# A two-layer kernel: second batch's norm statistics, normalised tiles, gating and last layer's weights put in other slots of the row loop

## The chip, the cores and the metric

One core of a Trainium2 chip runs the whole kernel in one launch. A core has a matrix engine (PE, with weight loads shown as PEld), a vector engine (DVE), an activation engine (ACT), a general engine (POOL) and a queue engine that issues transfers (SP). The metric is the device time in microseconds, and the figure for a kernel is the median of several runs.

## The reference, cut to what matters

The input x has 2 batches of 1024 rows of 512 numbers. There are two layers, and each layer adds an attention part and a second part, both computed from the same normalised input:

```python
x = L0_attn_x
xn = _layernorm(x)
x = x + L0_attn(xn) + L0_ffn(xn)      # one head of 128; streams mixed by a 4x4 Sinkhorn matrix per row
xn = _layernorm(x)
x = x + L1_attn(xn) + L1_ffn(xn)      # 32 heads in 8 groups, causal; gated experts of rank 16
```

In `L0_ffn` each row's 512 numbers are 4 streams of 128. A matrix `H_res` per row (50 rounds of row and column normalisation of 16 logits) mixes the streams, and a small branch is added. `L1_attn` projects to 32 query heads and, over a latent of 4 x 128 columns, to 8 key and value heads; scores are masked causally. `L1_ffn` is a gate and a product:

```python
h = relu(layernorm(xf @ gw1.T + gb1) * ln_gamma + ln_beta)
gates = h @ gw2.T + gb2
top_v, top_i = top_k(gates, 2);  top_g = softmax(top_v)
counts = onehot(top_i).sum(0);   allowed = counts <= capacity     # over both batches
w = onehot * top_g * allowed
out = xf @ weight.T + lora_B(lora_A(xf) * w) / 16
```

The counts run over all 2048 rows, so that no routing weight is known before both batches have been gated.

## The kernel before, in words

All matrix products are made of 16-bit halves: a float32 operand is split into a high and a low part, and `mm3` (line 88) sums three products, high by high, high by low, low by high. A split of activations is a high part on ACT and a low part on DVE (`evac`, lines 104 and 105); a split of weights is three POOL instructions (`split_pool`, lines 94 to 96: a scaling, a high part, a low part).

A tile is 128 rows of x; a batch has 8. `acc[b, t]` holds the running sum of tile t of batch b. Layer 0 of both batches comes first (`front0`, `attn0_rows`, `branch0`, `attn0_out`), with the mixing of the first batch's streams and its second norm. Then comes `layer1_attn`, which is most of the time.

`layer1_attn` runs over 16 groups g (8 of the first batch, then 8 of the second) and 32 row steps s in each. A row step takes 32 query rows of 4 heads against the keys so far (`row_step`): score matmuls on PE (tile `s`, 32 to 1024 columns), a row minimum on DVE (lines 283 and 287, into `P`), the exponential on ACT (line 291), a reciprocal (302), the high part on ACT (308) and the low part on DVE (314), both into `Phl`, and a transpose by DMA on SP (line 320, `PT<-Phl`). Rows lag: `row_step` finishes the row before the one whose scores it starts. `last_low` names the newest low part. In the first 8 rows of a group four rows share a `P` and a `Phl` buffer, in the next 8 rows two do, later each has its own; POOL sets the unused columns of `Phl` to zero (line 319).

All else is put between row steps. `at(g, s, f)` and `put(h, s, f)` name the slot after which a piece is written down; `put` counts from `8 * h`, so slot 200 is group 6, row 8. Group work has fixed slots: keys and values, query projections (`xT` by `wq`, evacuated at lines 104 and 105), the products with the transposed rows (`av`, line 345), and the output projection (`wo_block`), whose result is added to `acc` at line 737 on DVE, which frees its `pp` buffer; there are three of those (`BP`). The slots of what is not group work are in the constants at the top: `SK0, SKN` the second batch's Sinkhorn steps, `MX0, MXN` its mixing, `LN1` its second norm, `G0` and `G1` the gating of the first and second batch with `GL` slots between a tile and its gating matmul, `WT` the routing weights, `LX` the tiles of the second batch's `xT`, `LA` its latents, `FW` the last layer's weights, `FF` its first blocks. All of these lie in groups 0 to 7.

The order within each engine's queue is then set by the scheduler of the language, from what is written in the slots and from dependencies; it may put an instruction earlier or later than its slot. Two helpers bind it: `tc.issue_after`, and `behind(i, j, wait)`, which puts i behind j, with `wait` through a semaphore even across engines. POOL's weight splits (`parts_of`, `ffn_split`) and the adds of the mixing (line 634) wait in this way for the newest low part.

What the change touches:

- `mix0_units(1, t, ...)`: loads x again, scales it on POOL (617), and for each of 4 streams makes four ACT copies scaled by `Hm` (633) and one POOL add into `acc` (634).
- `layernorm_tiles`: `bn_stats` and an aggregation per tile (219, 220), then a square root by logarithm and exponential with corrections (`rsqrt`), and the scales `rs` (223, 224), for all 8 tiles in slot `LN1`.
- `normed_T`: scales a tile (`pool` chooses DVE 237, POOL 235 or ACT 233), its high part on ACT (238), its low part on POOL (240) or DVE, and a DMA transpose on SP (242). `tile_of` does this for the second batch's gating, scaling on POOL into `f2k` with high and low parts in `xr` (4 buffers) and the result in a `wo` buffer; the transposed tiles are dropped after gating, because `xT` (one buffer) still holds the first batch. `xT_tile` does it again when `xT` is free.
- `gating_h`: 12 matmuls of 32 columns (`gw`) and one DVE instruction (864) per tile; `gating`: DVE work for all 8 tiles in ten steps (lines 868 to 913).
- `weights_of`: sums the counts of both batches with a matmul (919) and makes the routing weights on DVE (921 to 929). `ffn_block`: one tile of the last product.
- `lat_w`, `ffn_fetch`, `ffn_split`: loads on POOL's queue and splits of the latent and last layer's weights.

## Time and profile before

| what | us |
|---|---|
| median of 3 runs (lowest to highest) | 1857.18 (1856.16 to 1858.09) |
| the profiled execution's own time | 1855.46 |
| its span, first to last instruction | 1853.7 |
| PE, DVE, ACT, POOL busy | 1715.7, 1447.6, 1194.1, 910.6 |
| group 6 (rows 192 to 223): length, PE busy in it | 122.15, 107.61 |
| group 9 (nothing but group work): length, PE busy in it | 91.79, 91.79 |

Lines such as L314 are lines of the kernel above. An instruction group is written out<-in with the program's tile names. Busy time is the time in which an engine executes; the idle time before an instruction is put down to what released it last, and where the engine named had been done for long, it was another, often a DMA. The granted clock is the share of its full clock that PE got.

### The profile page before, as it was taken

How to read it: one execution, taken by the hardware profiler on the slowest of the kernel's cores; microseconds unless marked ns; L12 is line 12 of the kernel's file. 1: busy time of each engine (PE TensorE's matmuls, PEld its weight loads, DVE VectorE, ACT ScalarE, POOL GpSimd, SP SyncE). 2: the span in 40 equal slices, each digit the busy share in tenths (PEclk: the TensorE clock that was granted, in tenths of full speed). 3: DMA queues.
4: the chain of work that ended last, by engine and by line, in shares of the span. 5: the costliest groups of instructions: out<-in, count | busy, mean ns of one | idle time of the engine just before them, and what ended most of it. 6: DMA issues, size and time to landing. Idle time of an engine off the chain costs nothing. (4 is left out here: it accounts for less than half of the span.)

```text
span 1853.7 us, 35094 instructions
## 1 busy us (share of the span) xinstructions
PE 1715.7 (93%) x11458; PEld 1046.0 (56%) x11458; DVE 1447.6 (78%) x4050; ACT 1194.1 (64%) x2917; POOL 910.6 (49%) x1540
## 2 busy tenths in 40 slices
PE   4756399999999999998999999999999999999998
PEld 3434146566666556655555556666666666656565
DVE  8888978988888877777976867777777777777675
ACT  3848665656676778776544756666666767676554
POOL 5567639768775455647634333424242433335200
PEclk9878699999999999999999999999999999999999
DMA  7435225666574657468546555656565656566455
GB/s 211 82 56 124 67 51 131 143 115 144 113 147 102 143 115 158 111 131 158 137 92 141 130 120 126 146 111 150 107 151 115 142 117 140 117 141 139 101 123 120
DMA packets 707306, 230.26 MB, mean 124 GB/s; under 512 B 689953, under 2 KB 690081, under 8 KB 707122
## 3 DMA queue, kind: packets, MB, share of 16 engines
q1 hardware_dynamic: 691666, 180.75, 47.2%
q0 software_dynamic: 13152, 43.07, 8.5%
q10 hardware_dynamic: 2304, 4.20, 0.7%
q8 instruction: 90, 1.47, 0.4%
q14 instruction: 94, 0.77, 0.1%
HBM read 52.81 MB, written 4.19 MB: 31 GB/s over the span
## 5 line engine op out<-in xcount | busy, mean ns | idle before, releaser
L291 ACT ACTIVATE P<-P,nm 128x1024 f32<-128x1024 f32 (+31 forms) x528 | 391.3, 742 | 250.0 <-DVE nm L283 234.8
L314 DVE SCALAR_TENSOR_TENSOR Phl<-P,r,Phl 128x1024 f16<-128x1024 f32 (+31 forms) x515 | 434.4, 853 | 85.9 <-ACT Phl L308 79.5
L88 PE MATMUL s<-K,Q 128*128 128x512 f16 (+22 forms) x2400 | 440.7, 317 | 19.5 <-DVE P L287 11.6
L345 PE MATMUL av<-PT,V 128*128 128x256 f16 x3648 | 447.7, 274 | 7.5 <-DMA PT<-Phl 6.8
L345 PEld LDWEIGHTS <-V 128*128 128x128 f16 x3648 | 357.0, 98 | 94.7 <-DMA PT<-Phl 8.3
L308 ACT ACTIVATE Phl<-P,r 128x1024 f16<-128x1024 f32 (+31 forms) x515 | 370.0, 731 | 22.3 <-DMA PT<-Phl 3.3
L88 PE MATMUL pp<-xT,wq 128*128 128x512 f16 x1536 | 372.9, 381 | 6.3 <-DVE acc L737 3.2
L88 PE MATMUL pp<-wo,ao 128*128 128x512 f16 x1536 | 369.9, 379 | 2.9 <-ACT ao L104 2.7
L94 POOL TENSOR_SCALAR f2k<-f2k 128x512 f32<-128x512 f32 x164 | 109.5, 668 | 499.9 <-DVE Phl L314 444.5
L88 PEld LDWEIGHTS <-Q 128*128 128x128 f16 x2400 | 223.2, 98 | 178.2 <-issue 28.4
L88 PEld LDWEIGHTS <-wq 128*128 128x128 f16 x1536 | 149.6, 98 | 173.8 <-issue 8.5
L88 PEld LDWEIGHTS <-ao 128*128 128x128 f16 x1536 | 149.4, 98 | 156.5 <-ACT ao L104 4.8
L287 DVE TENSOR_SCALAR_CACHE_REDUCE P<-s 128x512 f32<-128x512 f32 (+15 forms) x272 | 152.6, 562 | 21.7 <-PE s L88 19.7
L283 DVE CUSTOM_DVE_ANT_0 P<-s,mask,nm 128x272 f32<-128x272 f32 (+15 forms) x256 | 157.3, 615 | 8.7 <-PE s L88 1.0
L303 ACT ACTIVATE r<-r 128x1 f32<-128x1 f32 x528 | 96.2, 193 | 66.2 <-DVE r L302 65.4
L319 POOL MEMSET Phl<- 128x192 f16 (+2 forms) x384 | 72.6, 209 | 133.5 <-DMA PT<-Phl 95.7
L302 DVE RECIPROCAL r<-r 128x1 f32<-128x1 f32 x528 | 79.2, 155 | 75.3 <-ACT P L291 72.1
L104 ACT ACTIVATE ao<-av 128x512 f16<-128x512 f32 x128 | 75.1, 587 | 92.2 <-PE av L345 92.0
L283 DVE CUSTOM_DVE_ANT_0 P<-s,mask 128x32 f32<-128x32 f32 (+15 forms) x256 | 104.3, 432 | 27.6 <-PE s L88 27.1
L104 ACT ACTIVATE Q<-pp 128x512 f16<-128x512 f32 x128 | 74.5, 582 | 76.7 <-PE pp L88 72.2
L737 DVE SCALAR_TENSOR_TENSOR acc<-pp,acc 128x512 f32<-128x512 f32 x128 | 87.4, 682 | 41.0 <-PE pp L88 40.6
L105 DVE SCALAR_TENSOR_TENSOR Q<-pp,Q 128x512 f16<-128x512 f32 x128 | 87.6, 684 | 34.9 <-ACT Q L104 34.6
(254 smaller groups left out, 2119.1 us busy)
## 6 DMA issues: line engine op xcount, KB each, us to landing
f2k<-in_Wq POOLq DMA_DIRECT2D x64, 256.0 KB, 3.2
f2k<-in_WoT POOLq DMA_DIRECT2D x64, 256.0 KB, 3.3
PT<-Phl SPq DMA_TRANSPOSE x528, 3.2
acc<-in_x SPq DMA_DIRECT2D x16, 256.0 KB, 4.6
f2k<-in_Wup POOLq DMA_DIRECT2D x16, 256.0 KB, 3.5
out<-acc ACTq DMA_DIRECT2D x16, 256.0 KB, 3.5
xr<-in_x SPq DMA_DIRECT2D x12, 256.0 KB, 4.1
f2k<-in_Wlat POOLq DMA_DIRECT2D x8, 256.0 KB, 5.5
```

The source lines that it names most:

```text
L88: nc.tensor.matmul(dst, lhs(l), rhs(r), start=(i == 0 and j == 0), stop=(i == n - 1 and j == 2))
L94: first = G.tensor_scalar(stage, stage, scale, 1.0, ALU.mult, ALU.mult)
L104: A.activation(hl_hi, src, AF.Copy, scale=scale)
L105: return V.scalar_tensor_tensor(hl_lo, src, scale, hl_hi, ALU.mult, ALU.subtract)
L283: last_row[0] = V.tensor_tensor_reduce(Pm[:, o:o + w], pt[:, :w], mask[:, 512 - w:], -scale, first, ALU.add, ALU.min, nm[:, k:k + 1])
L287: last_row[0] = V.tensor_scalar(Pm[:, o:o + w], pt[:, :w], -scale, first, ALU.mult, ALU.min, accum_out=nm[:, k:k + 1])
L291: A.activation(Pm[:, :W], Pm[:, :W], AF.Exp, bias=last, scale=-1.0, accum_out=r[:, 0:1])
L303: A.activation(r[:, 1:2], r[:, 1:2], AF.Copy, scale=PSCALE)
L308: A.activation(hl[:, 0, :W], Pm[:, :W], AF.Copy, scale=r[:, 1:2])
L314: lo = V.scalar_tensor_tensor(hl[:, 1, :W], Pm[:, :W], r[:, 1:2], hl[:, 0, :W], ALU.mult, ALU.subtract)
L345: nc.tensor.matmul(p, Vh(j, l), PT(r * nj + j), start=(j == 0 and k == 0), stop=(j == nj - 1 and k == 2))
L737: V.scalar_tensor_tensor(acc[b, t], p, 1.0 / 256.0, acc[b, t], ALU.mult, ALU.add)
```

## The change

The statistics of each tile of the second batch are written three slots after its last mixing unit, and slot `LN1` holds only the scales. Mixing takes 65 slots from 119 instead of 74 from 122. A normalised tile of the second batch is written in two slots: scaling and high part in the first, low part and transpose in the next (`later`), and where POOL does either, it waits for the newest low part of a row. Tiles 1, 4 and 7 of the gating are scaled on ACT (`GP`). The gating tiles have slots of their own (`G1`), their matmuls three slots on, and the ten gating steps start at `G2`. The first batch's gating starts at slot 6 instead of 16. The last layer's weights have a list of slots (`FW`), the first blocks and the routing weights are one slot later, and the latent weights are loaded two slots ahead of their split, which waits for a low part.

```diff
--- before.py
+++ after.py
@@ -37,12 +37,15 @@
 FP = ((0, 2, 0, 2, 0, 2, 0, 2), (2, 2, 2, 2, 2, 2, 2, 2))
 X1 = 7
 CA, CB, CC, CD = 4, 1, 1, 3
-SK0, SKN, MX0, MXN, LN1 = 1, 116, 122, 74, 198
-
-G0, G1, GL, WT, LX, LA = 16, 200, 3, 220, 231, 240
+SK0, SKN, MX0, MXN, LN1 = 1, 116, 119, 65, 187
+
+G0, GL, WT, LX, LA = 6, 2, 221, 231, 240
+G1 = (198, 199, 200, 201, 203, 204, 205, 207)
+GP = (1, 2, 1, 1, 2, 1, 1, 2)
+G2 = 210
 AVD, WOD = 5, 10
 KVN, QN, QNN, QH = 19, 18, 24, 1
-FW, FF = 210, 221
+FW, FF = ((210, 212, 213, 215, 216, 218), tuple(8 * 58 + 2 + 2 * k for k in range(6))), 222
 BS, BP, BV = 4, 3, 1
 CQ, CV = (0, 1), (0, 0)
 PSCALE = 16384.0
@@ -211,20 +214,24 @@
         rs = C(f"rs{tag}{b}", [P, 3, NT])
         return mv, rs
 
-    def layernorm_tiles(b, mv, rs, ts):
+    def layernorm_tile(b, mv, t):
+        st = T("bnst", [P, 6], bufs=2)
+        V.bn_stats(st, acc[b, t])
+        V.bn_aggr(mv[:, t, :], st)
+
+    def layernorm_tiles(b, mv, rs, ts, stats=True):
         ve = T("ve", [P, NT], bufs=2)
         sl = slice(ts[0], ts[-1] + 1)
-        for t in ts:
-            st = T("bnst", [P, 6], bufs=2)
-            V.bn_stats(st, acc[b, t])
-            V.bn_aggr(mv[:, t, :], st)
+        for t in ts if stats else ():
+            layernorm_tile(b, mv, t)
         V.tensor_scalar(ve[:, sl], mv[:, sl, 1], LN_EPS, None, ALU.add)
         rsqrt(rs[:, 0, sl], ve[:, sl], "rs")
         V.tensor_scalar(rs[:, 2, sl], rs[:, 0, sl], 4.0, None, ALU.mult)
         return V.scalar_tensor_tensor(rs[:, 1, sl], mv[:, sl, 0], -1.0, rs[:, 2, sl],
                                       ALU.mult, ALU.mult)
 
-    def normed_T(b, mv, rs, t, dst, pool, tags=(("f2k", FB), ("wo", WB))):
+    def normed_T(b, mv, rs, t, dst, pool, tags=(("f2k", FB), ("wo", WB)), later=None):
+
 
         xn = T(tags[0][0], [P, NC, P], bufs=tags[0][1])
         xf = xn.rearrange("p c d -> p (c d)")
@@ -232,14 +239,25 @@
         if pool > 1:
             A.activation(xf, acc[b, t], AF.Identity, scale=rs[:, 2, t:t + 1], bias=rs[:, 1, t:t + 1])
         elif pool:
-            G.tensor_scalar(xf, acc[b, t], rs[:, 2, t:t + 1], rs[:, 1, t:t + 1], ALU.mult, ALU.add)
+            xg = G.tensor_scalar(xf, acc[b, t], rs[:, 2, t:t + 1], rs[:, 1, t:t + 1], ALU.mult, ALU.add)
+            if later is not None:
+                behind(xg, last_low[0], True)
         else:
             V.tensor_scalar(xf, acc[b, t], rs[:, 2, t:t + 1], rs[:, 1, t:t + 1], ALU.mult, ALU.add)
         last_hi[0] = A.activation(hl[:, :, 0, :], xn, AF.Copy)
         eng = G if pool in (1, 2) else V
-        lo = eng.tensor_tensor(hl[:, :, 1, :], xn, hl[:, :, 0, :], ALU.subtract)
-        (last_pool if eng is G else last_lo)[0] = lo
-        last_T[0] = nc.sync.dma_start_transpose(dst, hl.rearrange("p c l d -> p (c l d)"))
+
+        def low():
+            lo = eng.tensor_tensor(hl[:, :, 1, :], xn, hl[:, :, 0, :], ALU.subtract)
+            if eng is G and later is not None:
+                behind(lo, last_low[0], True)
+            (last_pool if eng is G else last_lo)[0] = lo
+            last_T[0] = nc.sync.dma_start_transpose(dst, hl.rearrange("p c l d -> p (c l d)"))
+
+        if later is None:
+            low()
+        else:
+            later(low)
 
     def proj_T(w, xT, half):
 
@@ -672,12 +690,8 @@
     def latents(b):
         cmp[b] = T("cmp", [P, NC, 2, S], F16, bufs=1)
 
-    def lat_w(mc):
-        st = T("f2k", [P, NC, P], bufs=FB)
-        nc.gpsimd.dma_start(st, a["Wlat"][mc])
-        w1 = T("wo", [P, 2, NC, P], F16, bufs=WB)
-        split_pool(st, w1[:, 0], w1[:, 1], 32.0)
-        return w1
+    def lat_w(st):
+        return parts_of(st, "wo", 32.0, WB).rearrange("p l (c d) -> p l c d", c=NC)
 
     def fetch(src):
         st = T("f2k", [P, 512], bufs=FB)
@@ -999,13 +1013,13 @@
     def new_xT(b):
         xT1[b] = T("xT", [P, NT, 2 * NC, P], F16, bufs=1)
 
-    def xT_tile(b, t, pool):
+    def xT_tile(b, t, pool, later=None):
         normed_T(b, *ln1[b], t, xT1[b][:, t], pool, (("f2k", FB), ("wo", WB)) if b else
-                 (("xr", XB), ("wo", WB)))
-
-    def tile_of(b, t):
+                 (("xr", XB), ("wo", WB)), later)
+
+    def tile_of(b, t, later):
         d = T("wo", [P, 2 * NC, P], F16, bufs=WB)
-        normed_T(b, *ln1[b], t, d, True, (("f2k", FB), ("xr", XB)))
+        normed_T(b, *ln1[b], t, d, GP[t], (("f2k", FB), ("xr", XB)), later)
         return d
 
     new_xT(0)
@@ -1035,9 +1049,13 @@
     gw1 = gating_w()
     chain = sinkhorn(1, logit[1])
 
+    def late_stats(t):
+        if t == 0:
+            ln1[1] = layernorm(1, "b")
+        layernorm_tile(1, ln1[1][0], t)
+
     def late_norm():
-        ln1[1] = layernorm(1, "b")
-        layernorm_tiles(1, *ln1[1], range(NT))
+        layernorm_tiles(1, *ln1[1], range(NT), False)
 
     extra = {}
 
@@ -1055,6 +1073,7 @@
     for t in range(NT):
         for k, f in enumerate(mix0_units(1, t, f0[1][5], True)):
             put(0, MX0 + MXN * (4 * t + max(k - 1, 0)) // 32, f)
+        put(0, MX0 + MXN * (4 * t + 3) // 32 + 3, lambda t=t: late_stats(t))
     for t in range(NT):
         put(1, 2 * t, lambda t=t: branch0_add(1, t, y4s[t], f0[1][4]))
     hs, gates, dts, lw = {}, {}, {}, {}
@@ -1066,21 +1085,25 @@
     def gate_step(b):
         next(gates[b], None)
 
-    for b, s in ((0, G0), (1, G1)):
+    lows = {}
+
+    for b, s in ((0, G0), (1, G1[0])):
         put(0, s, lambda b=b: gate_start(b))
         for t in range(NT):
             if b == 0:
                 put(0, s + t, lambda t=t: gating_h(hs[0], t, gw1, xT1[0][:, t]))
             else:
-                put(0, s + t, lambda t=t: dts.update({t: tile_of(1, t)}))
-                put(0, s + t + GL, lambda t=t: gating_h(hs[1], t, gw1, dts[t]))
+                put(0, G1[t], lambda t=t: dts.update({t: tile_of(1, t, lambda f: lows.update({t: f}))}))
+                put(0, G1[t] + 1, lambda t=t: lows.pop(t)())
+                put(0, G1[t] + GL + 1, lambda t=t: gating_h(hs[1], t, gw1, dts[t]))
         for k in range(10):
-            put(0, s + NT + GL + k, lambda b=b: gate_step(b))
+            put(0, (G2 if b else s + NT + GL) + k, lambda b=b: gate_step(b))
     put(0, LN1, late_norm)
     put(0, WT, weights_of)
     put(0, LX, lambda: new_xT(1))
     for t in range(NT):
-        put(0, LX + t, lambda t=t: xT_tile(1, t, t % 2 == 1))
+        put(0, LX + t, lambda t=t: xT_tile(1, t, t % 2 == 1, lambda f: lows.update({t: f})))
+        put(0, LX + t + 1, lambda t=t: lows.pop(t)())
 
     def lat_unit(mc, th):
         if mc + th == 0:
@@ -1088,13 +1111,14 @@
         lat_evac(1, mc, th, lat_block(1, lw[mc], th))
 
     for mc in range(4):
-        put(0, LA + 2 * mc - 4, lambda mc=mc: lw.update({mc: lat_w(mc)}))
+        put(0, LA + 2 * mc - 6, lambda mc=mc: lw.update({mc: fetch(a["Wlat"][mc])}))
+        put(0, LA + 2 * mc - 4, lambda mc=mc: lw.update({mc: lat_w(lw[mc])}))
         for th in range(2):
             put(0, LA + 2 * mc + th, lambda mc=mc, th=th: lat_unit(mc, th))
     for k in range(6):
-        for s in (FW, 8 * 58 + 2):
-            put(0, s + 2 * k - 2, lambda k=k: ffn_fetch(k))
-            put(0, s + 2 * k, lambda k=k: ffn_split(k))
+        for s in FW:
+            put(0, s[k] - 2, lambda k=k: ffn_fetch(k))
+            put(0, s[k], lambda k=k: ffn_split(k))
     for t in range(NT):
         put(0, FF + t, lambda t=t: ffn_block(0, t))
         put(60, 4 * t + 3, lambda t=t: ffn_block(1, t))
```

## The prediction

> **What bounds the kernel now.** I read the page's busy times first, then busy time by stage, then the waits of the stages that fall behind. A stage is one group of layer 1 (its first score matmul, 32 columns wide, marks the start); groups 0 to 9 start at the times in this windows view:
>
> ```profile
> PE 1715.7 (93%) x11458; PEld 1046.0 (56%) x11458; DVE 1447.6 (78%) x4050; ACT 1194.1 (64%) x2917; POOL 910.6 (49%) x1540
> ...
> 261.86:353.17 91.31, 90.09 (x697) 56.38 (x697) 82.87 (x235) 59.57 (x151) 68.10 (x118) 1.00 0.49 114
> 353.17:451.68 98.51, 95.13 (x620) 58.26 (x618) 84.68 (x255) 63.77 (x155) 73.63 (x161) 0.98 0.65 139
> ...
> 634.08:729.12 95.04, 92.04 (x612) 56.68 (x611) 77.45 (x198) 73.28 (x196) 54.45 (x80) 1.00 0.66 141
> 729.12:823.86 94.74, 93.60 (x621) 57.59 (x620) 73.42 (x196) 75.56 (x209) 53.80 (x78) 1.00 0.58 126
> 823.86:946.01 122.15, 107.61 (x784) 67.28 (x782) 102.57 (x277) 72.54 (x175) 82.51 (x116) 0.96 0.70 146
> 946.01:1086.09 140.08, 137.33 (x861) 78.29 (x862) 97.19 (x250) 75.42 (x183) 48.01 (x77) 1.00 0.54 119
> ...
> 1178.11:1269.90 91.79, 91.79 (x614) 56.98 (x612) 69.73 (x189) 60.89 (x149) 33.91 (x62) 1.00 0.61 128
> ```
>
> The columns after the length are PE, PEld, DVE, ACT, POOL busy, then the granted clock. In group 9 PE is busy all the time: nothing but less matmul work helps there. Length less PE busy is what could be won: 1.2, 3.4, 1.0, 0.7, 3.0, 1.1, 14.5 and 2.8 us in groups 0 to 7 (groups 2 and 3 from the same view), 27.7 us in all. More than half lies in group 6, where the second batch's tiles are normalised, gated, and the last layer's weights are split. The change edits this stretch, the mixing before it and the first batch's gating. So the bound is PE, short of its operands for 14.5 us in one group, and everything else is off the path. The waits of group 6, in two stretches:
>
> ```profile
> PE pp L88 <- DVE acc L737: 3.2, 1, 3.2
> ...
> PE pp L88 <- DVE Phl L314: 2.7, 1, 2.7
> ...
> PE s L88 <- DVE P L287: 1.7, 1, 1.7
> ...
> PE pp L919 <- DVE ch L913: 1.3, 1, 1.3
> PE pp L88 <- POOL cmp L95: 0.8, 1, 0.8
> ...
> L314 DVE SCALAR_TENSOR_TENSOR Phl<-P,r,Phl 128x480 f16<-128x480 f32 x1 | 2.0, 1977 | 0.0
> L314 DVE SCALAR_TENSOR_TENSOR Phl<-P,r,Phl 128x416 f16<-128x416 f32 x1 | 1.9, 1914 | 0.0
> ...
> L314 DVE SCALAR_TENSOR_TENSOR Phl<-P,r,Phl 128x416 f16<-128x416 f32 x1 | 0.7, 652 | 0.0
> ```
>
> The 3.2 us (PE idle from 854.0): a q projection waits for a PSUM buffer that L737 is to free; L737 stands on DVE behind low parts (L314) which take 1.98 and 1.91 us here, and 0.65 for the 416 columns in group 9 (last row). POOL is in tile steps and weight splits without a break from 851.4 to 858.5. The 2.7 us at 874.8: the gating matmul of tile 5. DVE's Phl had long been done; the tile's transpose, third of three on SP from 867.4, was issued at 870.1 and landed at 877.4, when three 256 KB weight loads were issued from 870.3 to 875.5. The last three are DVE's backlog (19.9 of 20 us busy in 900 to 920 and in 920 to 940) and weights split late. After each gap the clock falls, to 0.57 in 856 to 860 and 0.63 in 876 to 880.
>
> **Statistics tile by tile.** No instruction is added or removed: 8 bn_stats (0.68 us) and 8 aggregations (0.17) either way, and the built order of before has them already at rows 128 to 195, each when its tile is mixed. The changed order has them at rows 124 to 181, and the scales done at row 182 instead of 199. Worth 0 by itself: rows hide 0.85 us each. It only means that POOL's first tile (it waited 0.95 us at 845 for rsb L224) no longer waits.
>
> **Mixing in 65 slots, not 74.** The same 32 units of four ACT copies (L633: 122 of them 38.7 us busy in 622 to 838) and a POOL add (L634, 1.28 us), 14% denser, 3 rows earlier and done 12 rows earlier. ACT is busy 176 of 220 us in 620 to 840; in the steady groups 0.66 of the time, so mixing is about 0.14 and becomes 0.16. ACT stays under 0.85 on average, but at the head of each group, where rows are short for PE and not for ACT, demand exceeds PE's: summing each built order at the trace's median per form, rows 168 to 171 need 10.9 us of ACT against 4.6 of PE (before at worst 7.9 against 2.9, rows 136 to 139). I take a loss of 1.5 us over groups 3 to 5 (bounds 5 and none; near the least, since these groups lose only 4.8 in all now). For it the head of group 6 is free of mixing: the gaps at 827.0 and 829.6 (1.6 and 0.3) sit there, and I take a gain of 1.5.
>
> **Tiles in two steps, three of them on ACT.** POOL: 5 tile scalings instead of 8 (0.76 to 1.1 us each in this stretch), 8 low parts of 1.15 as before. ACT: 3 scalings of 0.81 (row of L233), 2.4 us more where ACT has 50 us idle in the group. All 13 POOL steps now wait for a row's low part on DVE, and behind a waiting step stand POOL's weight splits and the zeroing of Phl, on SP the tile's transpose and then the rows' PT transposes, on ACT the tile's high part and then the exponentials. What pays is the slack. Before, transposes stand on SP after rows 202, 202, 202, 207, 207, 207, 208, 208 and their gating matmuls on PE after rows 207, 207, 208, 210, 210, 210, 211, 211: for the last five, 3 rows. Changed: 199, 199, 201, 201, 204, 205, 205, 207 against 206, 207, 207, 207, 208, 210, 210, 211: 4 rows or more for all. A row is some 3 us, so the 4 us by which the landing of 877.4 came later than a usual 3.3 is mostly covered: minus 2.7, and 0.9 for the clock behind it (0.37 of the 2.5 us busy in 876 to 880). With only two tiles at a time, transposes no longer come in threes.
>
> Does the wait cure the stretched low parts? Row: over rows 122 to 195, where mix adds already wait for low parts in just this way, low parts still took 13.6 us more than the same widths in groups 9 to 14, nearly all of it in rows 0 to 15 of a group (8.2 us in rows 120 to 143, 0.5 in 144 to 159), where low parts come two to four in a row and the next one meets the POOL step that the last one released. The tiles stand in rows 198 to 207, rows 6 to 15 of group 6. [...] By the row, the mix adds' rate (13.6 us over 31 adds, 0.44 each, with all else that runs there) would give 5.7. I take the row: contention from 6.8 to 5.7, and of the 3.2 us wait I count 1 as gone, no more. Tile part: 2.7 + 0.9 + 1 = 4.6, less 0.6 for ACT's high parts that wait for POOL: 4.0 (bounds -7 and 9: the listed gaps 0.8, 3.2, 2.7 and clock 2.4).
>
> **Gating and weights.** Second batch: the ten gating steps are 18.4 us of DVE (lines 868 to 913 in 880 to 946), now at rows 209 to 219 instead of 211 to 220. DVE demand less PE demand in rows 212 to 219 goes from 6.0 to 5.2 us. The weights of the last layer are split by slot 218 instead of 220 and its first block is at 222 instead of 221, so the 0.8 (cmp L95) goes; the routing weights' 1.3 and the 0.7 behind them (al L921) stand a slot further from their use and I count half. 0.8 + 0.8 + 1.0 = 2.6; I write 2.5 (bounds -2 and 6).
>
> First batch, gating from slot 6 instead of 16: the same DVE work, from rows 24 to 43 to rows 16 to 25. In rows 20 to 43 DVE demand exceeds PE's by 5.5 us before, and groups 0 and 1 lose 4.6: the sum is a fair gauge. Changed it is 3.4 in the same rows, a gain of 2; but rows 16 to 31 alone are 9.5 over (60.0 against 50.5), a loss of 4 if the matmuls put ahead of row 16 do not cover it. I take 0 (bounds -4 and 2).
>
> The second xT tiles and latent weights in group 7: the same loads two slots earlier, splits and odd tiles behind low parts; its 2.8 us of gaps stay (bounds -2 and 1.5).
>
> **Sum.** -1.5 + 1.5 + 4.0 + 2.5 + 0 + 0 = 6.5 us. The profiled execution took 1855.46 (span 1853.7 and 1.8 around it), so 1849.0 on its own scale; the median of the runs shown is 1.72 above it, so 1850.7.
>
> **Rivals.**
> (1) All of group 6 clears: 14.5 us of gaps less 1.2 that the first blocks' DVE chain keeps, and about 0.7 of clock, 14 us: 1843. For it: the slack above. Against: rows 212 to 219 stay DVE-bound.
> (2) The change does not do what it says: the statistics were spread already, the wait on low parts only moves the contention within the same rows, and DVE's backlog is the same 18.4 us. The 2.7 goes and 1.5 to 3 come back in the mixing and in group 0: 1857.
> [...]
>
> **How the numbers follow.** What a measurement of this kernel can tell from no change is about 0.2%, 3.7 us: faster is below 1853.5, slower above 1860.9. Forecast as summed 0.52, with 1846 to 1855 as its own range (0.44 faster, 0.08 within); (1) 0.13; (2) 0.11; (3) 0.24. So faster 0.57, same 0.19, slower 0.24. The range reaches to 1843 and over the slower case: 1842 to 1862.5.
>
> **What would show it.** Right: in group 6 (from 32 columns to 32 columns) a length near 115 us, no gating matmul waiting over 1 us, low parts of rows 198 to 207 still over their group 9 times by 4 to 7 us in sum, gaps in groups 3 to 5 up by 1 to 2. Groups 9 to 14 at 91.8 as before. Wrong: gating matmuls still waiting for a transpose; ACT idle before its high parts by over 1.5 us each; groups 0 and 1 losing over 8 us; or group 6 at 122.

## The result, and the profile after

| | before | changed |
|---|---|---|
| median of runs on one chip, in turn | 1858.09 us (7 runs, 1853.9 to 1861.58) | 1866.19 us (7 runs, 1863.07 to 1868.93) |
| ratio to before, 95% interval | | 1.0043 [1.0028, 1.0058] |
| span of the profiled execution | 1853.7 us | 1864.4 us |

The changed kernel is slower by 8 us, where 6.5 us of gain were forecast. The time lies above the range too. The groups of layer 1 in the changed kernel, first its busy row from the page, then busy time by stage (0, 1, 2, then 3 to 7; columns as in the prediction: length, then PE, PEld, DVE, ACT and POOL busy, granted clock, DMA share, GB/s):

```profile
PE 1722.7 (92%) x11458; PEld 1047.0 (56%) x11458; DVE 1450.9 (78%) x4050; ACT 1197.5 (64%) x2920; POOL 895.9 (48%) x1537
...
261.50:364.57 103.07, 94.81 (x702) 57.20 (x702) 95.99 (x274) 61.76 (x157) 69.27 (x127) 0.97 0.56 118
364.57:457.69 93.12, 92.11 (x614) 57.09 (x612) 75.50 (x219) 61.31 (x150) 73.16 (x161) 1.00 0.63 125
457.69:553.18 95.49, 92.58 (x610) 57.28 (x608) 77.14 (x221) 61.29 (x150) 61.72 (x144) 0.98 0.60 128
553.18:646.00 92.82, 92.82 (x618) 57.34 (x616) 77.15 (x214) 65.47 (x165) 55.57 (x114) 1.00 0.58 123
646.00:742.51 96.51, 93.22 (x610) 56.96 (x607) 73.67 (x195) 77.49 (x211) 55.70 (x80) 0.98 0.59 128
742.51:842.50 99.99, 95.70 (x617) 57.86 (x615) 77.44 (x207) 75.03 (x200) 52.08 (x80) 0.97 0.65 130
842.50:954.03 111.53, 101.49 (x743) 62.62 (x741) 95.02 (x260) 69.94 (x166) 65.45 (x102) 0.97 0.70 146
954.03:1096.38 142.35, 139.37 (x886) 80.19 (x885) 99.99 (x253) 75.48 (x183) 50.53 (x79) 1.00 0.52 116
```

Group 6 is 10.6 us shorter than before (122.15), which is even more than the 6.5 forecast for the whole. The loss is elsewhere: group 0 is 11.8 us longer (91.31 before), and groups 3, 4 and 5 are 3.5, 1.5 and 5.3 us longer. Matmul work moves over a group's border when the order changes (PE counts differ), so I add the lengths by stage. A is groups 0 to 2 (first batch's gating), B groups 3 to 5 (most of the mixing), C groups 6 and 7 (tiles, gating, weights, new `xT`). Groups 8 to 14 take the same in both kernels. Most of what follows rests on these sums, in us; the last two columns are the measured times.

| kernel | A | B | C | A+B+C | median (runs) | ratio to before |
|---|---|---|---|---|---|---|
| before | 282.9 | 279.1 | 262.2 | 824.2 | 1858.09 (7) | |
| changed | 291.7 | 289.3 | 253.9 | 834.9 | 1866.19 (7) | 1.0043 [1.0028, 1.0058] |
| e1: changed, first gating at 16 | 282.9 | 290.6 | 254.5 | 828.0 | 1858.94 (10) | 1.0004 [0.9992, 1.0016] |
| e2: changed, old mixing | 290.0 | 279.1 | 269.8 | 838.9 | 1864.14 (5) | 1.003 [1.0016, 1.0043] |
| e3: both of these | 283.2 | 279.0 | 267.5 | 829.7 | 1859.53 (10) | 1.0003 [0.9991, 1.0015] |
| e4: before, first gating at 6 | 292.9 | 279.2 | 264.7 | 836.9 | 1868.63 (4) | 1.0048 [1.0031, 1.0065] |
| e5: e1, mixing 3 slots later | 283.0 | 280.1 | 264.6 | 827.7 | 1859.09 (10) | 1.0002 [0.9983, 1.002] |
| e6: before, mixing of the change | 283.1 | 288.4 | 254.3 | 825.7 | 1857.55 (1) | |
| e7: e1, POOL steps without waits | 283.1 | 288.4 | 260.2 | 831.7 | 1864.01 (1) | |
| e8: before, gating matmuls at 6 | 288.6 | 281.1 | 262.4 | 832.2 | 1863.82 (1) | |
| e9: before, mixing as in e5 | 282.9 | 280.1 | 255.8 | 818.8 | 1853.64 (9) | 0.997 [0.9959, 0.9981] |
| e10: e5, group 7 as before | 282.9 | 280.1 | 264.4 | 827.5 | 1861.8 (10) | 1.001 [0.9997, 1.0022] |
| e11: before, first gating at 12 | 286.4 | 279.0 | 267.4 | 832.8 | 1864.61 (10) | 1.0025 [1.0014, 1.0036] |
| e12: e9 and tiles in two steps | 283.1 | 280.3 | 264.2 | 827.7 | 1857.18 (10) | 1.0005 [0.999, 1.0021] |
| e13: e9, first gating at 20 | 284.3 | 280.6 | 257.5 | 822.4 | 1856.41 (10) | 0.9994 [0.9985, 1.0004] |

Times of different rows are compared by their ratios, since each ratio is taken to runs of the kernel before that were made in turn with that row's own (medians 1857.96 to 1860.26). The sums come from one execution each. Between kernels that do the same in a stage, A repeats within 0.3 us with the first gating at 16, but only within 2.9 with it at 6 (changed, e2, e4); B repeats within 2.2 (e1 against e6 and e7) and C within 5.2 (before, e4, e8 and e11). The profiled executions of e2, e3 and e12 were 4.9, 5.1 and 6.3 us longer than the medians of their runs, and that of e10 4.9 shorter, so their sums have to be read together with the ratios. Layer 1 begins between 260.5 and 266.2 us in the profiled executions, and no change touches what is ahead of it; that part is left out of the sums.

Lines of the changed kernel have numbers 3 to 18 higher than the same lines of the kernel printed above: L91 is L88 there, L107 and L108 are L104 and L105, L301 is L283, L305 is L287, L309 is L291, L326 is L308, L332 is L314, L363 is L345, L635 and L651 are L617 and L633, L878 is L864.

### The profile page after: what moved, and what is told of

It is laid out like the page before. It is cut to its first block, busy times and chain, and to the rows that moved or that the text cites. A ratio compares the mean times of both kernels' runs of the same rounds, so it can differ in the third digit from the quotient of the medians.

```text
span 1864.4 us, 35112 instructions
## 1 busy us (share of the span) xinstructions
PE 1722.7 (92%) x11458; PEld 1047.0 (56%) x11458; DVE 1450.9 (78%) x4050; ACT 1197.5 (64%) x2920; POOL 895.9 (48%) x1537
## 4 chain that ended last, share of the span: by engine, by line
PE 52%; DVE 3%; DMA 2%; ACT 2%; issue 1%; POOL 1%; SPq 0%; POOLq 0%; ACTq 0%; DVEq 0%
PE pp L91 28%; PE av L363 13%; PE s L91 11%; DVE Phl L332 1%; DMA PT<-Phl 1%; ACT f2k L651 1%; ACT P L309 1%; DVE P L301 1%; ACT Phl L326 0%; DMA f2k<-in_Wlat 0%; DMA xT<-wo 0%; DVE P L305 0%; DMA twT<-twhl 0%; DMA wo<-xr 0%; POOL acc L652 0%
## 5 line engine op out<-in xcount | busy, mean ns | idle before, releaser
L309 ACT ACTIVATE P<-P,nm 128x1024 f32<-128x1024 f32 (+31 forms) x528 | 391.2, 741 | 259.0 <-DVE nm L301 246.7
L332 DVE SCALAR_TENSOR_TENSOR Phl<-P,r,Phl 128x1024 f16<-128x1024 f32 (+31 forms) x515 | 431.4, 849 | 95.3 <-ACT Phl L326 86.1
L91 PE MATMUL s<-K,Q 128*128 128x512 f16 (+22 forms) x2400 | 443.6, 318 | 24.3 <-DVE P L305 14.6
L363 PE MATMUL av<-PT,V 128*128 128x256 f16 x3648 | 447.2, 274 | 8.1 <-DMA PT<-Phl 6.7
L363 PEld LDWEIGHTS <-V 128*128 128x128 f16 x3648 | 356.6, 98 | 95.8 <-DMA PT<-Phl 8.0
L326 ACT ACTIVATE Phl<-P,r 128x1024 f16<-128x1024 f32 (+31 forms) x515 | 369.8, 731 | 18.8 <-DMA PT<-Phl 2.5
L91 PE MATMUL pp<-xT,wq 128*128 128x512 f16 x1536 | 378.4, 385 | 3.1 <-DVE K L108 1.8
L91 PE MATMUL pp<-wo,ao 128*128 128x512 f16 x1536 | 371.1, 380 | 2.8 <-ACT ao L107 2.6
L91 PEld LDWEIGHTS <-Q 128*128 128x128 f16 x2400 | 223.6, 98 | 183.0 <-issue 36.0
L91 PEld LDWEIGHTS <-wq 128*128 128x128 f16 x1536 | 151.3, 99 | 175.4 <-issue 15.6
L91 PEld LDWEIGHTS <-ao 128*128 128x128 f16 x1536 | 149.6, 98 | 156.1 <-ACT ao L107 5.6
L305 DVE TENSOR_SCALAR_CACHE_REDUCE P<-s 128x512 f32<-128x512 f32 (+15 forms) x272 | 152.3, 562 | 20.8 <-PE s L91 18.7
L301 DVE CUSTOM_DVE_ANT_0 P<-s,mask,nm 128x272 f32<-128x272 f32 (+15 forms) x256 | 157.8, 617 | 12.6 <-PE s L91 4.7
L301 DVE CUSTOM_DVE_ANT_0 P<-s,mask 128x32 f32<-128x32 f32 (+15 forms) x256 | 104.6, 432 | 28.7 <-PE s L91 27.7
L107 ACT ACTIVATE ao<-av 128x512 f16<-128x512 f32 x128 | 75.2, 587 | 80.3 <-PE av L363 80.0
L107 ACT ACTIVATE Q<-pp 128x512 f16<-128x512 f32 x128 | 74.5, 582 | 71.2 <-PE pp L91 67.5
L108 DVE SCALAR_TENSOR_TENSOR Q<-pp,Q 128x512 f16<-128x512 f32 x128 | 87.4, 683 | 27.5 <-ACT Q L107 27.3
```

The source lines that it names most:

```text
L91: nc.tensor.matmul(dst, lhs(l), rhs(r), start=(i == 0 and j == 0), stop=(i == n - 1 and j == 2))
L107: A.activation(hl_hi, src, AF.Copy, scale=scale)
L108: return V.scalar_tensor_tensor(hl_lo, src, scale, hl_hi, ALU.mult, ALU.subtract)
L301: last_row[0] = V.tensor_tensor_reduce(Pm[:, o:o + w], pt[:, :w], mask[:, 512 - w:], -scale, first, ALU.add, ALU.min, nm[:, k:k + 1])
L305: last_row[0] = V.tensor_scalar(Pm[:, o:o + w], pt[:, :w], -scale, first, ALU.mult, ALU.min, accum_out=nm[:, k:k + 1])
L309: A.activation(Pm[:, :W], Pm[:, :W], AF.Exp, bias=last, scale=-1.0, accum_out=r[:, 0:1])
```

## The experiments

**e1 to e4: the three parts taken apart.** e1 puts the first batch's gating back, e2 the mixing, e3 both; e4 makes only the gating early in the kernel before.

```diff
# e1 (against the changed kernel); e3 has both edits
-G0, GL, WT, LX, LA = 6, 2, 221, 231, 240
+G0, GL, WT, LX, LA = 16, 2, 221, 231, 240
-            put(0, (G2 if b else s + NT + GL) + k, lambda b=b: gate_step(b))
+            put(0, (G2 if b else s + NT + 3) + k, lambda b=b: gate_step(b))
# e2 (against the changed kernel)
-SK0, SKN, MX0, MXN, LN1 = 1, 116, 119, 65, 187
+SK0, SKN, MX0, MXN, LN1 = 1, 116, 122, 74, 197
# e4 (against the kernel before)
-G0, G1, GL, WT, LX, LA = 16, 200, 3, 220, 231, 240
+G0, G1, GL, WT, LX, LA = 6, 200, 3, 220, 231, 240
-            put(0, s + NT + GL + k, lambda b=b: gate_step(b))
+            put(0, s + NT + (GL if b else 2) + k, lambda b=b: gate_step(b))
```

> The changed kernel with only the first batch's gating put back (starts at slot 16, three slots before its steps). Theory (early gating lost the time at the start): groups 0 and 1, 196.2 us in the changed kernel and 189.8 before, go back to about 190, and the whole comes to about 1860; group 2 stays at 95.5 if its own loss has another cause and falls to 93 if it is a tail of the early gating. Rival (the denser mixing or the tile steps lost it all, the start differs by chance of the scheduler): groups 0 and 1 stay above 194.

> The changed kernel with only the mixing put back to 74 slots from slot 122 (scales in slot 197). Theory (denser mixing lost 7 us in groups 3 to 5): groups 4 and 5, 196.5 us in the changed kernel and 189.8 before, go back to about 190, while group 6 gives back part of its gain, since mixing ends in it again: whole about 1861. Rival (the loss is not of the mixing's density but of the tile steps and waits): groups 4 and 5 stay above 195.

> The changed kernel with both put back: first batch's gating at 16 and mixing in 74 slots; left of the change are the tiles in two steps, the second gating's slots and the last layer's weights. Theory (these three alone are a gain, as forecast): 6 us below the kernel before, about 1851, with group 6 at 112 to 116. Rival (group 6 gained only because mixing left it earlier): group 6 at 120 or more and the whole at 1857 or above.

> The kernel before with only the first batch's gating moved to slot 6 (steps two slots behind its matmuls). Theory (early gating alone costs 6 us): groups 0 and 1 from 189.8 to about 196, whole about 1864. Rival (it costs only together with the other moves): within 2 us of before.

With the gating back at 16, stage A is 282.9, exactly as before (e1); with the gating alone early it is 292.9 (e4). So the first batch's gating costs 7 to 10 us in stage A, and the ratio of the change falls from 1.0043 to 1.0004 without it: nearly all of the measured loss. With the old mixing, stage B is 279.1 again (e2), so the denser mixing costs 10 us there. What is left of the change when both are taken out (e3) gains nothing: its ratio is 1.0003, where 6 us below before were expected.

**Why the early gating costs.** The windows view of e4 shows in its first line where the time goes:

```profile
265.25:368.05 102.80, 94.88 (x702) 57.19 (x702) 96.02 (x274) 61.69 (x157) 69.28 (x127) 0.97 0.55 119
```

DVE is busy for 96.0 us in group 0. Before it was 82.9, and the group lasted 91.3, so that DVE alone now needs more than the group took. All ten gating steps (18.9 us of DVE by their lines in the changed trace) now run in group 0; before, 8.4 us of them did. Where the queue jams first is seen in the changed kernel's timeline (start, duration, engine, line; in brackets the idle time before it and what ended it):

```profile
276.48 0.46 PE L91 MATMUL pp<-gw,xT 128*128 128x32 f16 x12
...
277.29 2.51 DVE L332 SCALAR_TENSOR_TENSOR Phl<-P,r,Phl 128x320 f16<-128x320 f32 x1
277.45 0.46 PE L91 MATMUL pp<-gw,xT 128*128 128x32 f16 x12
...
279.72 0.68 DVE L108 SCALAR_TENSOR_TENSOR K<-pp,K 128x512 f16<-128x512 f32 x1
...
280.45 0.81 PE L91 MATMUL pp<-xT,wq 128*128 128x512 f16 x3 [1.79 <-DVE K L108]
```

The gating matmuls of two tiles (12 each) take two of the three `pp` buffers ahead of the query projection, and the third is freed only when DVE has done a low part and then the keys. In the built order before, that projection (12 matmuls of 512 columns) stood at row 11 and the gating matmuls came from row 16. All waits of PE in 277 to 300 are of this kind:

```profile
PE pp L91 <- DVE K L108: 1.8, 1, 1.8
PE pp L91 <- DVE Q L108: 1.6, 1, 1.6
PE pp L91 <- DVE xr L878: 0.6, 1, 0.6
```

Later in the group DVE itself is behind. In 301.5 to 349.5 us it is busy for 47.7 of 48 us (44.0 in 301.9 to 349.9 of before), and at its end PE waits for a row minimum (L305). These are the longest of its waits in 340 to 366:

```profile
PE s L91 <- DVE P L305: 1.9, 1, 1.9
PE pp L91 <- ACT ao L107: 1.2, 1, 1.2
```

**e8 and e11: is it the matmuls' place, or coming early?** e8 moves only the matmuls to slot 6 and leaves the ten steps at slot 27. e11 moves both by four slots, so that the matmuls stay behind the query projection of row 11.

```diff
# e8
-        put(0, s, lambda b=b: gate_start(b))
+        put(0, s if b else 6, lambda b=b: gate_start(b))
-                put(0, s + t, lambda t=t: gating_h(hs[0], t, gw1, xT1[0][:, t]))
+                put(0, 6 + t, lambda t=t: gating_h(hs[0], t, gw1, xT1[0][:, t]))
# e11
-G0, G1, GL, WT, LX, LA = 16, 200, 3, 220, 231, 240
+G0, G1, GL, WT, LX, LA = 12, 200, 3, 220, 231, 240
```

> The kernel before with the first batch's gating matmuls at slots 6 to 13 and its ten DVE steps left at slots 27 to 36. If early gating costs by the steps' DVE work, which falls where rows 16 to 31 leave DVE no room: groups 0 and 1 stay at 190 here (195.9 with both early). If it costs by the matmuls, their PSUM buffers and the order they force: 194 or more.

> The kernel before with the first batch's gating four slots earlier (12, not 16): its matmuls now stand behind the query projection that is followed in group 0's row 11, and the ten gating steps from slot 23. Theory (gating from slot 6 costs because its matmuls take the three pp buffers ahead of the query projections of rows 11 to 13): groups 0 and 1 together 189.8 to 191 as before (195.9 from slot 6), group 2 at 93.1 (97.0), ratio 1.000. Rival (earlier gating costs by coming earlier, into rows where DVE is short): about four tenths of the loss, groups 0 and 1 at 192 to 193 and group 2 above 94, ratio 1.0015 to 1.002.

PE's waits in 277 to 366 us, first of e8, then of e11:

```profile
PE s L88 <- DVE P L287: 2.5, 1, 2.5
PE pp L88 <- DVE K L105: 1.8, 1, 1.8
PE pp L88 <- DVE Q L105: 1.6, 1, 1.6
PE pp L88 <- ACT ao L104: 1.5, 1, 1.5
PE pp L88 <- DVE xr L864: 0.6, 1, 0.6
```

```profile
PE s L88 <- DVE P L287: 5.0, 3, 2.4
PE s L88 <- DVE nm L283: 2.0, 2, 1.6
PE pp L88 <- ACT ao L104: 0.4, 1, 0.4
```

e8 has the same three `pp` waits to a tenth (4.0 us), so the matmuls' place makes them; the 194 us or more expected for this case in groups 0 and 1 came as 195.9. e11 has none of them, so my theory is right about these three. But e11 isn't free: groups 0 and 1 take 193.2 us against 189.8, because PE waits for the row minima (L287, L283), with which DVE is behind, instead. The theory said 189.8 to 191 and fell; the rival's 192 to 193 was near. So there are two causes, a buffer queue in rows 11 to 16 and DVE behind with the rows later in group 0. They do not simply add up. e8 (one run) leaves the steps in place and loses 6.1 us in groups 0 and 1, just as much as e4, which moves both. The 4.3 us by which e4's stage A is longer than e8's lie in group 2 (97.0 us against 92.7; 95.5 in the changed kernel, 94.2 in e2, 93.1 in e1), where no gating work is left; what makes them is not settled.

**e13: is later better still?** The same gating at 20, on e9.

```diff
-G0, G1, GL, WT, LX, LA = 16, 200, 3, 220, 231, 240
+G0, G1, GL, WT, LX, LA = 20, 200, 3, 220, 231, 240
```

> The kernel before with the shifted mixing (which took 0.997 of the kernel before) and the first batch's gating four slots later, at 20. Theory (gating costs by coming early, 6.1 us in groups 0 and 1 from slot 6 and 3.4 from slot 12): groups 0 and 1 together 187.5 to 190 against 189.8, ratio 0.995 to 0.997. Rival (slot 16 is a balance, and DVE's backlog at the start of group 1 grows when the ten gating steps move into it): groups 0 and 1 at 192 or more, ratio 0.998 or more.

Groups 0 and 1 take 190.3 and stage A 284.3 against 282.9. That lies between the two expectations; the ratio, 0.9994, is the rival's. Slot 6 costs 9 to 10 us in stage A, 12 costs 3.5, 16 nothing and 20 costs 1.4: of these four slots 16 is the best, and the loss is not one of coming early as such.

**e5, e6 and e9: what the mixing costs, and gives.** e6 is the kernel before with the mixing of the change alone. e5 and e9 keep its 65 slots and begin three slots later, e5 in e1 and e9 in the kernel before.

```diff
# e6
-SK0, SKN, MX0, MXN, LN1 = 1, 116, 122, 74, 198
+SK0, SKN, MX0, MXN, LN1 = 1, 116, 119, 65, 198
# e9
-SK0, SKN, MX0, MXN, LN1 = 1, 116, 122, 74, 198
+SK0, SKN, MX0, MXN, LN1 = 1, 116, 122, 65, 190
# e5 (against e1)
-SK0, SKN, MX0, MXN, LN1 = 1, 116, 119, 65, 187
+SK0, SKN, MX0, MXN, LN1 = 1, 116, 122, 65, 190
```

> The kernel before with only the mixing in 65 slots from 119 (norm left in slot 198). If the mixing alone carries both effects: groups 3 to 5 from 279.0 to about 290 and group 6 from 122 to about 114. If the gain of group 6 needs the tiles in two steps too: groups 3 to 5 to 290 and group 6 at 118 or more.

> The changed kernel with the first batch's gating back at 16 and the 65 slots of mixing moved three slots later (from 122; scales in slot 190). A tile's load and first streams now stand at slots 122, 130, 138 and so on instead of 119, 127, 135, 143, 151, 159: none at the turn of a group. Theory (the turn: eight or sixteen copies on ACT in front of the last row's exponential and the first rows of the next group): groups 3 to 5, 290.6 us with the mixing at 119, come down to 280 to 283, group 6 stays at 110 to 113, whole about 1849. Rival (density: ACT has too much in 65 slots wherever it starts): groups 3 to 5 stay above 287 and the whole at 1857 or more.

> The kernel before with the mixing alone changed: 65 slots as in the change, but from slot 122 (not 119), the scales at 190. Theory (the mixing loses where its tiles' loads meet the last row of a group, not by being denser): groups 3 to 5 take 280 us together (before 279.1, mixing from 119 alone 288.4), group 6 takes 115 to 116 (before 122.2) since its head is free of mixing, group 7 stays at 139 to 140; span 1847 to 1849, ratio about 0.997. Rival A (density itself costs): groups 3 to 5 at 286 or more, span about 1855. Rival B (the shifted mixing is what put group 7 at 149.9 in the earlier run with this shift): group 7 at 147 or more, span about 1857.

The same density costs 9.3 us in stage B when it begins at 119 (e6, 288.4) and 1.0 us at 122 (e5 and e9, 280.1). e5's theory held in stage B and failed for the whole (1859.09 us, not 1849), since its group 7 took 149.9 us; e9's held but for group 6, which took 117.3 us instead of 115 to 116. What differs is the slots where a tile begins: 119 + 65 x 4t / 32 gives 127 and 159, the last rows of groups 3 and 4. The changed kernel's timeline, ACT and then POOL, and the wait on DVE that follows (view of the waits, 642 to 651) show what that does:

```profile
643.06 1.12 ACT L326 ACTIVATE Phl<-P,r 128x992 f16<-128x992 f32 x1
644.08 0.58 ACT L107 ACTIVATE Q<-pp 128x512 f16<-128x512 f32 x1
646.38 2.44 ACT L651 ACTIVATE f2k<-xr,Hm 128x128 f32<-128x128 f32 x8 [1.72 <-POOL xr L635]
648.73 1.13 ACT L309 ACTIVATE P<-P,nm 128x1024 f32<-128x1024 f32 x1
```

```profile
645.58 0.77 POOL L635 TENSOR_SCALAR xr<-xr,rsa 128x512 f32<-128x512 f32 x1 [3.71 <-DVE Phl L332]
```

```profile
DVE r L320 <- ACT P L309: 2.2, 1, 2.2
```

The tile's scaling on POOL waits 3.7 us for a low part, eight copies on ACT wait for the scaling, and the exponential of the last, 1024 wide row stands behind the copies in ACT's queue. From 644.7 to 648.7 ACT does nothing for a row. DVE waits 2.2 us for the exponential with the row's reciprocal, the next row minima stand behind that, and PE then waits for these minima: 2.8 us in 640 to 660, against 0.8 us at the same border of before (630 to 641). In e6 it is 2.8 us again, in e5 and e9 0.8. Sixteen copies stand on ACT between the high parts of the rows of 992 and 1024 columns in the change and in e6, none in e9.

What the mixing gives is seen in e9's groups 6 and 7, and in the gating matmuls of e9 against those of before (first answers of the view of the tile `gw`: durations, then first and last start):

```profile
827.58:944.88 117.30, 105.98 (x795) 66.09 (x792) 99.73 (x268) 68.63 (x164) 69.56 (x108) 1.00 0.68 145
944.88:1083.35 138.47, 134.88 (x840) 75.94 (x838) 94.07 (x248) 75.69 (x183) 49.82 (x77) 1.00 0.53 120
```

```profile
L88 PE MATMUL pp<-gw,wo x96: 176/176/207, 864.4 to 884.4; 128*128 128x32 f16 x96
```

```profile
L88 PE MATMUL pp<-gw,wo x96: 176/176/189, 858.6 to 877.4; 128*128 128x32 f16 x96
```

The first of these two is before, the second e9. From the starts of group 6 (823.9 and 827.6) the gating matmuls run at 40.5 to 60.5 us before and at 31.0 to 49.8 in e9, with tile code that is the same line for line. The scales of the norm were ready 20.9 us into group 6 before, and 15.6 us ahead of it in e9, and the same tile steps go some 10 us earlier. PE's idle time in group 6 falls from 14.5 to 11.3 us, and the granted clock goes from 0.96 to 1.00, which by itself is worth about 4.9 us by estimate (0.04 of 122.15). Stage C falls by 6.4 us (e9) and 7.9 us (e6). No run has the early scales without the moved mixing, so that the head of group 6, now free of mixing, is not parted from them. e9 is the version that beats both kernels: 0.997 [0.9959, 0.9981].

**e7, e10 and e12: what the two-step tiles are worth.** e7 is e1 with the same steps but without their waits for low parts. e10 is e5 with group 7 (new `xT`, latent weights) as before. e12 also has the old slots of the weights, routing weights, first blocks and gating steps, and so is e9 and the gating tiles of the change: two steps, their own slots, three scalings on ACT, statistics tile by tile.

```diff
# e7 (against e1)
-            if later is not None:
-                behind(xg, last_low[0], True)
-            if eng is G and later is not None:
-                behind(lo, last_low[0], True)
# e10 (against e5), with lat_w as before
-        put(0, LX + t, lambda t=t: xT_tile(1, t, t % 2 == 1, lambda f: lows.update({t: f})))
-        put(0, LX + t + 1, lambda t=t: lows.pop(t)())
+        put(0, LX + t, lambda t=t: xT_tile(1, t, t % 2 == 1))
# e12 (against e10)
-G0, GL, WT, LX, LA = 16, 2, 221, 231, 240
+G0, GL, WT, LX, LA = 16, 2, 220, 231, 240
-G2 = 210
+G2 = 211
-FW, FF = ((210, 212, 213, 215, 216, 218), tuple(8 * 58 + 2 + 2 * k for k in range(6))), 222
+FW, FF = (tuple(210 + 2 * k for k in range(6)), tuple(8 * 58 + 2 + 2 * k for k in range(6))), 221
```

> The changed kernel with gating back at 16 and without the waits of the tiles' POOL steps for low parts (order alone decides). If the waits keep POOL out of the low parts' way: low parts of rows 192 to 207 lose 6 us or more over their group 9 times (4.2 with the waits), and group 6 goes from 110.3 to 113 or more. If the waits do nothing or delay the tiles: group 6 within 1 us of 110.3 or shorter, and the gating matmuls' waits for a transpose, 2.7 us in sum, shrink.

> The changed kernel with the first batch's gating at 16 and the mixing from 122 (as the earlier run with both), and in group 7 the second xT tiles again in one step and the latent weights loaded and split at once, as before. Theory (what costs group 7 some 7.5 us there is the pair of steps that wait for low parts, with their transposes in one run ahead of the rows'): group 7 back from 149.9 to 140 to 142, other groups as in that run (group 6 at 114 to 116), span about 1848. Rival (group 7 is lost to what comes before it: gating, routing weights and last layer's weights in their new slots): group 7 at 147 or more, span about 1857.

> The changed kernel with the mixing from 122 and the first batch's gating at 16, and with group 7, the last layer's weights, the routing weights, the first blocks (221) and the gating steps (from 211) as before: against the kernel before with the shifted mixing it differs by the second batch's gating tiles in two steps alone. Theory (group 7 is lost to the first blocks and routing weights a slot later, which free the transposed tiles' buffer 3 to 4 us later): group 7 at 138 to 141 and the last read of the first batch's tiles 48 to 49.5 us into it; group 6 114 to 117; span 1848 to 1852, ratio 0.995 to 0.998. Rival (the gating tiles in two steps shift the later work by themselves): group 7 at 147 or more, span 1856 or more.

In no pair that differs by the tiles and what goes with them is stage C shorter: 0.2 us longer (e1 against e6), 5.0 (e2 against e4), 5.3 (e3 against before), 8.8 (e5 against e9), and 8.4 for the gating tiles alone (e12 against e9). The 5.0 and 5.3 are about the spread of C. The ratios, which stand on many runs, give 0.5 us of loss for e3 against before and 3 us of gain for e2 against e4 (their intervals overlap), but 6 to 6.5 us of loss for e5 and e12 against e9. So the tiles in two steps show a gain nowhere that is clear of noise, and a loss where the mixing begins at 122. The theory of e12 missed with group 6 (120.6 us), group 7 (143.6) and the ratio (1.0005); the rival's 147 for group 7 did not come either. e12's gating matmuls, and the two longest of PE's waits in its group 6:

```profile
L91 PE MATMUL pp<-gw,wo x96: 176/176/190, 854.1 to 883.5; 128*128 128x32 f16 x96
```

```profile
PE pp L91 <- DMA wo<-xr: 3.9, 3, 2.1
PE av L363 <- DMA PT<-Phl: 3.7, 3, 2.1
```

Group 6 begins at 829.7 here, so the gating matmuls run from 24.4 to 53.8 us into it, against 31.0 to 49.8 in e9 with tiles in one step: the first comes earlier and the last later. Three of them wait for their transpose, 3.9 us, which in e9 is 0.3 us in all. That does not settle it: e6, with tiles in one step too, has 3.0 us of these waits and a group 6 of 115.7 us, and 5.1 of the 8.4 us between e12 and e9 are in group 7 (143.6 against 138.5). What makes the tiles of the change slower stays open. The waits for low parts themselves are not shown to be the cost: without them (e7, one run), stage C is 5.7 us longer, not shorter.

Nor do the waits keep POOL out of the low parts' way. I compare each low part of rows 192 to 207 with the median of the same width in groups 9 to 14. The sixteen take 4.6 us more in e1, which has the waits, and 0.9 us more in e7, which has not (6 or more was expected if they helped); in e9 and e6, with tiles in one step, it is 1.8 and 2.6.

Group 7 is either 138 to 145 us long (before, changed, e1, e4, e6, e8, e9, e11, e12, e13) or 147 to 153 (e2, e3, e5, e7, e10). My theory for e10, that the two steps of the `xT` tiles make the difference, fell: it took 152.8. The view of the tile `xT` in 985 to 1025 has the symptom, first of e10, then of e9:

```profile
  DMA xT<-wo: 8.5, 2
...
DMA to landing us min/median/max: 3.1/5.2/9.6
```

```profile
  DMA xT<-wo: 1.3, 1
...
DMA to landing us min/median/max: 3.0/4.4/5.7
```

The transposed tiles land up to 9.6 us after their issue, and PE waits for two of them. In e12, with the weights and first blocks a slot earlier, group 7 is 143.6 and the long form is gone. But group 6 is 9 us longer than in e10 (120.6 against 111.6), so that the stage is the same (264.2 and 264.4). All long ones have the tiles in two steps, but the changed kernel and e1 have them too, with the late slots, and are short. What puts an order into the long form is not settled.

## Why the prediction was wrong, step by step

| step of the sum | forecast gain | measured |
|---|---|---|
| mixing in 65 slots, groups 3 to 5 | -1.5 (-5 to 0) | -9.3 (e6) |
| head of group 6 free of mixing | 1.5 | 7.9, all of stage C (e6); 6.4 (e9) |
| tiles in two steps; gating and weights of the second batch; group 7 | 6.5 | -0.2 in stage C (e1 against e6); by the ratios 3 (e2 against e4), -0.5 (e3 against before), -6 to -6.5 (e5 and e12 against e9) |
| first batch's gating | 0 (-4 to 2) | -8.8 in stage A (changed against e1); -10.0 (e4) |
| sum | 6.5 | -10.7 in the profiled executions, -8 by the ratio |

From before to e6 to e1 to the changed kernel A+B+C grows by 1.5, 2.3 and 6.9 us, 10.7 in all; of the 2.3, 2.2 are in stage B, where e6 and e1 do the same, and lie within its spread. Of e6's 9.3 and 7.9, some 1.6 us is matmul work that moved from stage C to B (by its columns, at the 0.42 ns of one in group 9).

- *First batch's gating.* This step failed by most. The forecast set DVE's demand of rows 20 to 43 against PE's and called the gain of 2 and the loss of 4 a tie "if the matmuls put ahead of row 16 do not cover it". They cover nothing and do harm themselves: they take `pp` buffers ahead of the query projection, a wait that the sum did not have at all (e8, which moves them alone, loses 6.1 us in groups 0 and 1). DVE's loss is real too (e11: 3.4 us there), and its demand should have been added over the whole group as well: 82.9 us of DVE before and 10.5 of gating steps more are 93.4, in a group of 91.3. But that sum is no sharp test: in e11 it is 87.6, and e11 loses all the same. The prediction's own sign, "groups 0 and 1 losing over 8 us", is what came: length less PE busy is 8.3 and 1.0 there.
- *Mixing.* The mechanism, ACT's copies ahead of a row's exponential, is right; the place and the size are not. The sum looked at rows 8 to 11 of a group, where demand is highest; the loss is at the last row, where eight copies must wait for a POOL step that waits for a low part. Summing demand misses a wait. The loss of clock was missed too: idle time rose by only 2.8 us in groups 3 to 5 (4.8 to 7.6, lengths less PE busy), while granted clocks of 0.98 and 0.97 where 1.00 was before are worth about 1.9 and 3.0 us more by estimate (share lost times the lengths); some 2.5 us of the 10.3 is matmul work that moved in, by its columns.
- *Statistics and the head of group 6.* "Worth 0 by itself" was wrong in what hangs on it. With the scales 36 us earlier the unchanged tile steps go some 10 us earlier, PE's wait behind L737 falls from 3.2 to 0.8 us, and the clock in group 6 stays at 1.00 (e9). That is far more than the two gaps at the head counted for 1.5, though no run parts the early scales from the free head.
- *Tiles in two steps.* The forecast worked out slack from the slots of the change against those of before, and so gave the tiles what the mixing gives. Group 6 came out at 111.5 us where "near 115" was to show it right, but e6 has 115.7 without any of it, and the whole stage C is the same (253.9 and 254.3): the sign came, and not for the forecast's reason. The transposes did not cease to be waited for: 2.7 us in two waits of the changed group 6, as much as in one before.

```profile
PE av L363 <- DMA PT<-Phl: 2.8, 1, 2.8
PE pp L91 <- DMA wo<-xr: 2.7, 2, 1.4
```

- *The slower case (3), at 0.24, and the tile part's lower bound, -7,* stood for low parts held up by POOL steps in group 6. No run shows a term of that size, on which the range's end at 1862.5 rests too. What the runs showed in its place: the low parts of rows 192 to 207 took 4.2 us more than the medians of the same widths in groups 9 to 14, where 5.7 was forecast, and 6.6 before by this measure (6.8 in the forecast). The time did come out slower, but by the first batch's gating (8.8 us in stage A) and the mixing (9.3 in stage B). The fall from 6.6 is no merit of the waits, since e7, e9 and e6 (0.9, 1.8 and 2.6) are lower without them.
- *Bounds.* Each term's bounds reached some way towards what came, but the slower cases were given one cause and 0.24. Two parts thought to be small carried some 18 us of loss between them (9.3 and 8.8), and one held 8 us of gain that was not seen.

## What to carry to other kernels

Before moving work of an engine into a stage, add it to what that engine does in the stage and compare with the stage's length. A sum above the length warned here (93.4 us in a group of 91.3, which grew by 11.8); one below it didn't clear the move (e11: 87.6, and the group grew by 5.6). Then ask which buffers it takes ahead of the critical work, not only how long it runs. When work is spread at a fixed step, look where each piece begins: three slots' shift took 8 us of loss away at the same density (stage B, e6 against e9). Take an input's lateness away before rewriting what consumes it; here, with the mixing done earlier, the old code was better than the new.

## What was not expected of the hardware

- Short gaps of PE went with a loss of clock nearly as large as the idle time in one group: in group 5 of the changed kernel PE is idle for 4.3 us (1.1 before) and the granted clock is 0.97, which by estimate (share lost times the length) is 3.0 of 100 us. In the changed group 0 the gaps at 344.9 and 348.7 are 1.9 and 1.2 us long, and the clock of the two windows from 341.5 is 0.90 and 0.67:

```profile
341.50:349.50 8.00, 5.16 (x30) 2.67 (x28) 8.00 (x25) 3.73 (x8) 6.16 (x10) 0.90 0.76 177
349.50:357.50 8.00, 7.63 (x32) 3.73 (x33) 6.36 (x22) 5.59 (x11) 5.06 (x12) 0.67 0.51 115
```

  The two gaps are 3.1 us of idle time; the clock of these rows is by estimate worth up to 3.4 us on top (0.10 + 0.33 of 8 us each). In narrower windows the same view gives 1.00 in 344.4 to 347.9 and 0.50 in 347.9 to 354.7, so that the clock fell about 1 us after the end of the gap of 1.9 us, and the second gap lies in the slow stretch. The matmuls of 512 columns of the query projection take 618 ns there in the mean, and 379 in group 9 of before. So half the clock followed a gap of 1.9 us here. It does not follow every such gap: PE's waits of 1.8 and 1.6 us in 277 to 300 of the same group left the clock at 1.00 (windows of 8 us from 277.5 to 301.5).
- The same 256 KB transposes land in 3.0 to 9.6 us. In e10 the tiles issued at 59.5 and 75.3 us of group 7 took 8.7 and 9.6 us, each overlapped by seven other transfers, loads and transposes; in e9 one issued with nothing in flight took 3.0. The number of others alone does not decide: in e10 one issued at 68.2 us with four in flight took 3.2.
- The start of layer 1 lies anywhere from 260.5 to 266.2 us between profiled executions, though no edit touches what is written ahead of it; a difference of two profiles' spans below some 5 us says nothing by itself.
